# A fused layernorm, causal attention and gated feed-forward kernel: the gate's multiplication, the last unit's diagonal blocks and the second sequence's layernorm take other places in the order of work

## The chip, the core and the metric

The kernel runs on one core of a Trainium2 chip, in a single launch. Its time is device microseconds, the median of several executions. Of one execution there is also a trace, taken by the hardware profiler. It names five engines: PE (TensorE, the matrix multiplications; PEld are its weight loads), DVE (VectorE), ACT (ScalarE), POOL (GpSimd) and SP (SyncE, which here issues nearly all transfers). Microseconds are written us.

## The reference

Two sequences of 1024 tokens with 512 features each, in fp32. Cut to what matters:

```python
xn = layernorm(x)                                   # x: (2, 1024, 512)
q, k, v = (xn @ W.T + b  for W, b in (q, k, v))     # 32 heads of 16
scores = q @ k.T / sqrt(16), causal
s = softmax(scores) @ v @ Wo.T + bo                 # the attention
base = xn @ W_base.T + b_base
w = top-2 of softmax(xn @ W_gate.T) over 8 experts, made to sum to 1
g = silu(base + sum_e w_e * (xn @ A_e.T) @ B_e.T)   # rank 16 each
out = x + s * g
```

## The kernel before

**Units and steps.** All of it is in `direct` (`general` is a second version for inputs out of range; it does not run here). A sequence is b = 0 or 1, and each has two chunks of 512 queries, c = 0 or 1. The 32 heads are four groups of eight (oc). A unit is one (b, oc, c), and there are 16. A unit of chunk 0 has 5 steps, one of chunk 1 has 13 steps; together 144 steps, n = 0 to 143, listed in `plan`. The first unit of the second sequence starts at step 72.

**What a step does.** `scores(n)` (L1610 on) multiplies queries and keys of four heads at once into two PSUM tiles s (the matmuls of L1624; 8 or 16 records of 512 or fewer columns), and ACT takes the exponential of each into a tile pt (128x1024, "exps" below). There are two s tiles, so the scores of step n+1 wait for the exps of step n, and three pt tiles, so the second exp of a step also waits until `values` of the step before has read its buffer. `values(n-1)` (L1676) then multiplies the previous step's pt with the values into the accumulators av. `masked(n)` (L1652) sets the upper triangle of diagonal blocks to zero on POOL, with affine_select. Last, `fill(n)` puts other work behind these: a share of the PE work of the tasks (projections of v, q, k, the gate, the output), planned so that every step gets about the same amount, and what goes with it on DVE, ACT and SP.

**Which blocks share a step.** A step takes pieces of key tile by queries, at most 512 columns. `unit_steps` is for all units but the last. `last_steps` (L1291) orders the last unit's 13 steps, n = 131 to 143. Diagonal pieces are those whose key tile and first query tile are the same. In its steps n = 137 and 138 the two pieces (key tile k0 with 384 columns, key tile k0+2 with 128 columns) are both diagonal.

**What sets the order inside `fill`** (L1513 on). The engines run their instructions in the order in which the program records them; `fill` records: 1. all of `turns` that is due; 2. the PE tasks with their DVE additions (a product's PSUM tile is emptied by such an addition; there are two of these tiles, so each product waits for the addition of the last but one); 3. `splits`; 4. all of `later` that is due (L1574); 5. `urgent` (`place_urgent`, which places queries and keys by DMA); 6. tasks without PE work, such as the layernorm, the sums of inputs and the routing. A task of the sixth kind may take its turn only when DVE is not behind by the planner's estimate (`enough`), unless its due step has come. `later` entries that wait for a DMA have an estimate of when it lands (`landed`).

**The gate** (`gate_task`, L887). The 512x512 block product is made by seven products (p1, p2, p6, p7, p5, p3, p4; Strassen's form) that leave four blocks of g. As each is complete, `final` puts `squash` into `later`: ACT makes sg = tanh(g/2) in a single buffer, and `multiply` (DVE, g = (sg + 1) * g) goes into `later` for the next step. If the next squash comes while a multiply is still pending, it is done first. There are four gates (b, c), with four blocks each: 16 tanh and 16 multiplications.

**The layernorm of a chunk** (`layernorm_task`, L293). SP loads x, DVE takes statistics of four tiles (bn_stats), normalizes four tiles and transposes them in 32x32 blocks (8 instructions, sq); each half goes to HBM (`store`, scr<-sq) and comes back in another order (`place`, four transfers xnT<-scr). The chunk (1,0) may begin from step 28 and is due at step 60 (s0 - 12 with s0 = 72). Its xnT is first used by the projection v of (1,0), which follows the queries and keys ("qk", 0, 1, 3) in the fixed order of stages.

Of the kernel before, what the change touches and what calls it, by code (L numbers as in the profile page):

```python
# [18 lines left out]
P = 128  # L19
# [78 lines left out]
def direct(ctx, tc, sound, x, wq, wk, wv, wo, wb, wa, wg, wB, bq, bk, bv, bo, bb, out):  # L98
# [28 lines left out]
    def chunk_tile(b, c):  # L127
        return sb.tile([P, TT, D], F32, tag="x", bufs=1, name=f"x_{b}_{c}")
# [63 lines left out]
    def load_rest():  # L192


        def by_rows(w):
            return w.rearrange("(kc p) o -> p kc o", p=P)

        for dst, src in (
            (wag_sb[:, :, 0:ER], by_rows(wa)),
            (wag_sb[:, :, ER:], by_rows(wg)),  # L200
            (wB_sb, wB),
            (bb_sb, bb.partition_broadcast(P)),
            (bo_sb, bo.partition_broadcast(P)),
        ):
            sp.dma_start(out=dst, in_=src)
# [42 lines left out]
    turned_at, now = {}, [0]  # L248
# [44 lines left out]
    def layernorm_task(b, c):  # L293


        xt = chunk_tile(b, c)
        for i in range(NS):
            i0 = c * C + i * P
            sp.dma_start(
                out=xt[i * SQ : (i + 1) * SQ],  # L300
                in_=x[b, i0 : i0 + P].rearrange("(t r) d -> r t d", r=SQ),
            )
        if b == 0:
            load_rest()
        tiles = [xt[:, t] for t in range(TT)]
        for _ in range(3 if b else 1):
            yield WAIT
        s = yield from statistics(tiles, True)
        if b:
            yield WAIT  # L310
        for t in range(0, TT, 2):
            normalize(tiles[t : t + 2], s[0][:, t : t + 2], s[1][:, t : t + 2])
            yield PAUSE
        if b:
            yield WAIT
        xnT = sb.tile([P, KC, C], F32, tag="xnT", bufs=3, name=f"xnT_{b}_{c}")
        for k0 in range(0, KC, 2):
            sq = sb.tile([P, 2, NS, TT, SQ], F32, tag="sq", bufs=1, name="sq")
            for t in range(TT):
                yield PAUSE  # L320
                ve.transpose(
                    out=sq[:, :, :, t],
                    in_=tiles[t][:, k0 * P : (k0 + 2) * P].rearrange(
                        "p (k q d) -> p k q d", k=2, q=NS
                    ),
                )
            scr = dram.tile([NS, SQ, 2, NS, TT * SQ], F32, tag="scr", name="scr")

            def store(sq=sq, scr=scr, place=None):
                sp.dma_start(  # L330
                    out=scr.rearrange("i d k q m -> (i d) (k q m)"),
                    in_=sq.rearrange("p k q t r -> p (k q t r)"),
                )
                if place:
                    landed(place, now[0] + 3)

            def place(k0=k0, scr=scr):
                for q in range(NS):
                    sp.dma_start(
                        out=xnT[q * SQ : (q + 1) * SQ, k0 : k0 + 2].rearrange(  # L340
                            "d k (i m) -> d k i m", i=NS
                        ),
                        in_=scr[:, :, :, q].rearrange("i d k m -> d k i m"),
                    )
                if k0:
                    turned_at[b, c] = now[0] + int((sp.landing() - sp.now) / 3.4)

            if not b:
                store()
                place()  # L350
                yield WAIT
                continue
            later.append((now[0] + b, lambda s=store, p=place: s(place=p)))
            for _ in range(0 if k0 else 1 + b):
                yield WAIT
        xnTs[b, c] = xnT
# [527 lines left out]
    def block_of(t):  # L884
        return lambda i, j: t[:, 2 * i : 2 * i + 2, BK * j : BK * j + BK]

    def gate_task(k):  # L887

        _, b, c = stages[k]
        gt = sb.tile([P, TT, D], F32, tag="g", bufs=1, name=f"g_{b}_{c}")  # L890
        away = (b, c) != (NB - 1, NC - 1)
        kept = dram.tile([P, TT, D], F32, tag="kept_g", name="kept_g") if away else None
        stored, multiplied = [], []
        g = block_of(gt)

        def more(ps, i, j, start):
            for t in range(2):
                matmul(
                    ps[:, t * BK : t * BK + BK],
                    lhsT=hwTs[b, c][:, :, 2 * i + t],  # L900
                    rhs=wB_sb[:, BK * j : BK * j + BK],
                    start=start and t == 0,
                    stop=t == 1,
                )

        def final(i, j):

            def squash():
                for x in [x for x in later if x[1].__name__ == "multiply"]:
                    later.remove(x)  # L910
                    x[1]()
                sg = sb.tile([P, 2, BK], F32, tag="tmp", bufs=1, name="sg")
                act.activation(sg, g(i, j), AF.Tanh, scale=0.5)
                later.append((now[0] + 1, lambda: multiply(sg)))
                later[-1][1].__name__ = "multiply"

            def multiply(sg):
                ve.scalar_tensor_tensor(g(i, j), sg, 1.0, g(i, j), ALU.add, ALU.mult)
                if away:
                    later.append((now[0] + 1, store))  # L920
                    return
                multiplied.append((i, j))
                if len(multiplied) == 4:
                    for t in range(TT):
                        gs[b, c * TT + t] = gt[:, t]

            def store():
                sp.dma_start(out=block_of(kept)(i, j), in_=g(i, j))
                stored.append((i, j))
                if len(stored) == 4:  # L930
                    g_tiles[b, c] = kept

            costs[squash] = (0.65, now[0] + 2)
            later.append((now[0] + 1, squash))

        yield from block_task(k, g, final, more)
# [212 lines left out]
        if posted.count(t) == 2:  # L1149
            turns.append((now[0] + 1, lambda: turn_last(b, c, t)))  # L1150

    needs = {}

    def landed(f, cap, at=None):

        needs[f] = sp.landing(), cap
        later.append((now[0] + 1 if at is None else at, f))

    turns, turned, posts, posted, later, patient, last_out = [], [], {}, [], [], [], []
# [131 lines left out]
    def last_steps(c):  # L1291

        k0, w = c * TT, C - P
        steps = []
        for par in range(2):
            for kt in range(0, k0, TT):
                for i in range(TT - 1):

                    steps.append([(par, kt + i, 0, w, 0), (par, kt + TT - 1, i * P, P, w)])
        steps += [[(par, k0, 0, w, 0), (par, k0 + 2, 2 * P, P, w)] for par in range(2)]  # L1300
        steps.append([(par, k0 + 1, P, 2 * P, 2 * P * par) for par in range(2)])
        keys = [k0 + TT - 1] + list(range(k0 + TT - 1))
        pieces = [(par, kt, w, P, i % 4 * P) for par in range(2) for i, kt in enumerate(keys)]
        return steps + [pieces[n : n + 4] for n in range(0, len(pieces), 4)]
# [8 lines left out]
    for u in units:  # L1313
        starts[u] = len(plan)
        steps = unit_steps(u[2]) if u != units[-1] else last_steps(u[2])
# [71 lines left out]
    for b in range(NB):  # L1387
        for c in range(NC):
            s0 = starts[b, 0, c]
            xn = [("xnT", b, c)]  # L1390
            if not b and not c:
                room["x"] -= 1
                Task(1, first_task(), 8 * MM, takes={"xnT": 1, "qT": 1, "kT": 1}, uses=xn)
            else:
                Task(
                    s0 - 12 if b else -9, layernorm_task(b, c), 0.0, after=s0 - (44 if c == 0 else 30) if b else -9,
                    takes={"x": 1, "xnT": 1}, frees={"x": 1},
                )
            turned_ = lambda u=(b, c): now[0] > turned_at.get(u, now[0]) + (0 if u[0] else 1)
# [59 lines left out]
            else:  # L1459
                before = starts[b, KC - 1, c] + 2  # L1460
                Task(len(plan) - 7, bases_task(b, c), 0.0, after=before - 12, takes={"xnT": 2})
                n = len(units) - 3
# [50 lines left out]
    def fill(n):  # L1513
# [54 lines left out]
        for x in [x for x in splits if x[0] <= n]:  # L1568
            if room["qT"] and room["kT"] and (calm(1.1) or n >= starts[x[2]] - 5):
# [1 line left out]
                room["qT"] -= 1  # L1571
                room["kT"] -= 1
                x[1]()
        for x in [x for x in later if x[0] <= n]:  # L1574
            if x not in later or x[0] == n and x[1] in patient and enough():
                continue
            lands, cap = needs.get(x[1], (0.0, 0))
            if lands > (begins if x[1] in patient else clock[0] + 1.0) and n < cap:
                continue
            if x[1] in costs and not calm(costs[x[1]][0]) and n < costs[x[1]][1]:  # L1580
                continue
            later.remove(x)
            x[1]()
# [21 lines left out]
    def place_urgent(n):  # L1605
        for x in [x for x in urgent if x[0] <= n]:
            urgent.remove(x)
            x[1]()
# [129 lines left out]
    while late or turns or tasks:  # L1738
        fill(last + 99)
# [463 lines left out]
```

## Time and profile before

| | |
|---|---|
| time, median of 3 (lowest to highest) | 549.01 us (548.78 to 549.1) |
| the profiled execution's own time | 548.63 us |
| its span, first to last instruction | 546.8 us |
| busy PE, DVE, ACT, POOL | 536.9, 333.0, 351.7, 117.9 us |
| granted TensorE clock, mean | 0.998 |
| transfers | 78.11 MB, mean 143 GB/s |
| exps (pt<-s) | 288, mean 1025 ns |
| masks (pt<-pt on POOL) | 224, mean 501 ns |

The span is what lies between the first and the last instruction; the profiled execution took 1.8 us more than its span. PE counts as busy while a matmul waits inside its group for a buffer, so its 98% hides short stalls: they are found by the distance from one step's first score matmul to the next step's, set against the work in the step. A projection or values matmul of the program stands as two records in the trace, so "p x32" is 16 matmuls; a score matmul stands as one.

### The profile page before, as it was taken

What the parts mean: (1) busy time and instruction counts of PE and PEld (TensorE: products, weight loads), DVE (VectorE), ACT (ScalarE), POOL (GpSimd) and SP (SyncE); (2) the same over time, 40 slices, a digit from 0 to 9 for tenths busy, and PEclk for the clock granted to TensorE, in tenths of its full rate; (3) what the DMA queues carried; (4) which work ended last, traced back from release to release, by engine and by line L of the source; (5) the groups of instructions that cost most, each with busy time, mean ns of one, the idle gap of its engine ahead of it and who ended that gap; (6) DMA issues with size and microseconds to landing.
All of it is one profiled execution on the core that took longest, in us unless ns stands there. A gap on an engine that the chain in (4) does not pass through costs nothing.

```text
span 546.8 us, 19460 instructions
## 1 busy us (share of the span) xinstructions
PE 536.9 (98%) x8411; PEld 278.3 (51%) x8411; DVE 333.0 (61%) x692; ACT 351.7 (64%) x390; POOL 117.9 (22%) x249
## 2 busy tenths in 40 slices
PE   8999999999999999999999999999999999999994
PEld 8435444554455544454645554454545554455562
DVE  4435586665575975576379766575176553648842
ACT  2437754776776867657667756657668767777531
POOL 2213401020134411030123321130123331020500
PEclk9999999999999999999999999999999999999999
DMA  8734357356527376813646545640123221652301
GB/s 262 183 101 159 133 161 233 99 177 197 175 99 230 120 243 209 220 42 100 199 153 197 187 131 176 198 137 23 64 99 123 86 75 46 232 172 86 99 22 66
DMA packets 66798, 78.11 MB, mean 143 GB/s; under 512 B 9880, under 2 KB 51872, under 8 KB 66064
## 3 DMA queue, kind: packets, MB, share of 16 engines
q1 hardware_dynamic: 66688, 76.78, 44.1%
q8 instruction: 68, 1.11, 0.8%
q14 instruction: 26, 0.21, 0.1%
q10 hardware_dynamic: 16, 0.00, 0.0%
HBM read 45.34 MB, written 19.37 MB: 118 GB/s over the span
## 4 chain that ended last, share of the span: by engine, by line
PE 95%; DVE 2%; ACT 1%; issue 0%; POOL 0%; ACTq 0%; POOLq 0%; DVEq 0%
PE av L1676 26%; PE p L257 23%; PE s L1624 18%; PE q L257 14%; PE ph L257 3%; PE pv L257 3%; PE po L257 2%; PE pk L257 1%; PE pq L257 1%; ACT pt L56 1%; PE warm L212 1%; PE pq_first L385 1%; PE h L257 1%; DVE g L56 1%; PE pk_first L385 1%
## 5 line engine op out<-in xcount | busy, mean ns | idle before, releaser
L56 ACT ACTIVATE pt<-s 128x1024 f32<-128x1024 f32 x288 | 290.4, 1025 | 151.8 <-PE s L1624 144.8
L1652 POOL TENSOR_SCALAR_AFFINE_SELECT pt<-pt 128x256 f32<-128x256 f32 (+1 forms) x224 | 108.6, 501 | 405.4 <-ACT pt L56 404.8
L1676 PE MATMUL av<-pt,v 128*32 128x512 f32 (+3 forms) x1680 | 155.7, 467 | 0.4 <-DVE v L56 0.2
L1624 PE MATMUL s<-qT,kT 32*128 32x512 f32 (+3 forms) x1616 | 108.2, 363 | 0.7 <-ACT pt L56 0.5
L1624 PEld LDWEIGHTS s<-qT,kT 32*128 32x128 f32 x1616 | 62.0, 183 | 59.4 <-issue 34.9
L1676 PEld LDWEIGHTS av<-pt,v 128*32 128x32 f32 x1680 | 41.1, 108 | 54.6 <-issue 38.8
L257 PE MATMUL p<-wt,asum 128*32 128x256 f32 x864 | 52.6, 379 | 0.0
L257 PE MATMUL q<-asum,wqk 128*32 128x256 f32 x832 | 51.1, 379 | 0.0
L257 PEld LDWEIGHTS p<-wt,asum 128*32 128x32 f32 x864 | 28.5, 110 | 26.4 <-issue 11.2
L257 PE MATMUL q<-xnT,wqk 128*32 128x256 f32 x624 | 39.5, 379 | 0.0
L257 PEld LDWEIGHTS q<-asum,wqk 128*32 128x32 f32 x832 | 26.8, 110 | 23.7 <-issue 7.2
L56 DVE TENSOR_TENSOR g<-p,g 128x512 f32<-128x512 f32 x20 | 13.8, 690 | 26.6 <-PE p L257 26.5
L257 PEld LDWEIGHTS q<-xnT,wqk 128*32 128x32 f32 x624 | 20.2, 110 | 18.5 <-issue 6.6
L56 DVE SCALAR_TENSOR_TENSOR kf<-q,kf 128x256 f32<-128x256 f32 x39 | 16.5, 424 | 21.3 <-PE q L257 20.6
L257 PE MATMUL p<-w,xnT 128*32 128x256 f32 x448 | 27.4, 379 | 0.0
L257 PE MATMUL p<-w,asum 128*32 128x256 f32 x320 | 20.8, 379 | 0.0
L257 PEld LDWEIGHTS p<-w,xnT 128*32 128x32 f32 x448 | 14.9, 110 | 10.6 <-issue 3.3
L257 PEld LDWEIGHTS ph<-wag_sb,xnT 128*32 128x32 f32 x512 | 15.3, 110 | 3.9 <-issue 3.0
L257 PE MATMUL ph<-wag_sb,xnT 128*32 128x136 f32 x512 | 16.6, 279 | 0.0
L56 DVE TENSOR_TENSOR x<-p,x 128x512 f32<-128x512 f32 x15 | 10.3, 688 | 10.3 <-PE p L257 10.2
L257 PE MATMUL po<-wo,oT 128*32 128x512 f32 x128 | 16.5, 592 | 0.0
L56 DVE TENSOR_TENSOR qT<-qf,qT 128x512 fp32r<-128x512 f32 x15 | 10.4, 696 | 9.4 <-ACT qT L56 9.4
(150 smaller groups left out, 565.8 us busy)
## 6 DMA issues: line engine op xcount, KB each, us to landing
wt<-kept SPq DMA_DIRECT2D x36, 256.0 KB
qT<-qT SPq DMA_DIRECT2D x30, 256.0 KB
x<-in_x_dram SPq DMA_DIRECT2D x16, 256.0 KB
kept<-wqk SPq DMA_DIRECT2D x16, 256.0 KB
wqk<-kept SPq DMA_DIRECT2D x4, 1024.0 KB
kT<-kf SPq DMA_DIRECT2D x30, 128.0 KB
scr<-sq SPq DMA_DIRECT2D x6, 512.0 KB
xnT<-scr SPq DMA_DIRECT2D x24, 128.0 KB
```

The costliest lines, as they stand in the source:

```text
L56: return getattr(self.engine, name)(*args, **named)
L212: nc.tensor.matmul(warm[:, n % 4 * P : n % 4 * P + P], lhsT=ident, rhs=ident, start=True, stop=True)
L257: nc.tensor.matmul(o[j : j + 32], lhsT=lhsT[:, j : j + 32] if len(lhsT.shape) == 2 else lhsT[:, j // 32], rhs=rhs, start=start, stop=stop,)
L385: nc.tensor.matmul(ps[:, cols], lhsT=w[:, k, :], rhs=xnT[:, k, cols], start=k == 0, stop=k == KC - 1)
L1624: nc.tensor.matmul(ss[s // 2][:, s % 2, col : col + w], lhsT=keys[rows, kt % TT * P : kt % TT * P + P], rhs=q[rows, halves * par + half_, ...
L1652: nc.gpsimd.affine_select(out=d, in_=d, compare_op=ALU.is_ge, fill=0.0, base=0, pattern=[[0, d.shape[1]], [1, P]], channel_multiplier=-1,)
L1676: nc.tensor.matmul(avs_now[par][32 * s : 32 * s + 32, q0 : q0 + w], lhsT=vs[b, kt][:, h * VS - HD * par : h * VS - HD * par + HP], rhs=pt[ ...
```

## The change

- `squash` puts `multiply` into `turns` and no longer into `later`. It is recorded at the start of the next step's `fill`, behind that step's `values` and ahead of the DVE additions of its products; before, it came behind them.
- In `last_steps` each diagonal piece is paired with one that isn't. For each half of the heads, the last of the three earlier steps gives its second piece away and takes the diagonal piece of key tile k0+2; the piece that it gave goes with the diagonal of k0 in a step that now directly follows. The four steps with one diagonal piece are then n = 133, 134, 137 and 138. The matmuls are the same.
- The layernorm of (1,0) is due at s0 - 25 = 47 in place of 60. (The chunk (1,1) keeps s0 - 12.)
- The `place` of a layernorm is named in `behind`. When `later` is worked off, such entries come last, and `urgent` is worked off ahead of each: xnT<-scr goes behind the placing of queries and keys on the SP queue.

```diff
@@ layernorm_task, store
                 if place:
+                    behind.append(place)
                     landed(place, now[0] + 3)
@@ gate_task, final
             def squash():
-                for x in [x for x in later if x[1].__name__ == "multiply"]:
-                    later.remove(x)
+                for x in [x for x in turns if x[1].__name__ == "multiply"]:
+                    turns.remove(x)
                     x[1]()
                 sg = sb.tile([P, 2, BK], F32, tag="tmp", bufs=1, name="sg")
                 act.activation(sg, g(i, j), AF.Tanh, scale=0.5)
-                later.append((now[0] + 1, lambda: multiply(sg)))
-                later[-1][1].__name__ = "multiply"
+                turns.append((now[0] + 1, lambda: multiply(sg)))
+                turns[-1][1].__name__ = "multiply"
@@
-    needs = {}
+    needs, behind = {}, []
@@ last_steps
                     steps.append([(par, kt + i, 0, w, 0), (par, kt + TT - 1, i * P, P, w)])
-        steps += [[(par, k0, 0, w, 0), (par, k0 + 2, 2 * P, P, w)] for par in range(2)]
+            steps.append([(par, k0, 0, w, 0), steps[-1][1]])
+            steps[-2][1] = (par, k0 + 2, 2 * P, P, w)
@@ tasks
                 Task(
-                    s0 - 12 if b else -9, layernorm_task(b, c), 0.0, after=s0 - (44 if c == 0 else 30) if b else -9,
+                    s0 - (12 if c else 25) if b else -9, layernorm_task(b, c), 0.0, after=s0 - (44 if c == 0 else 30) if b else -9,
@@ fill
-        for x in [x for x in later if x[0] <= n]:
+        for x in sorted((x for x in later if x[0] <= n), key=lambda x: x[1] in behind):
+            if x[1] in behind:
+                place_urgent(n)
             if x not in later or x[0] == n and x[1] in patient and enough():
                 continue
```

## The prediction

> **What bounds it now.** I read the page first: busy times and the chain that ended last.
>
> ```profile
> PE 536.9 (98%) x8411; PEld 278.3 (51%) x8411; DVE 333.0 (61%) x692; ACT 351.7 (64%) x390; POOL 117.9 (22%) x249
> PE 95%; DVE 2%; ACT 1%; issue 0%; POOL 0%; ACTq 0%; POOLq 0%; DVEq 0%
> ```
>
> PE sets the end nearly everywhere. The change takes no matmul away: in the built program the 32-column products are the same, 8 of them stand in other steps. So time can come only from steps in which PE waits. To find them I set the distance between the first score matmuls of neighbouring steps against the work between them. A full step (16 products, 32 records) takes 3.39 us and one with half of these 2.53, so a record of 256 columns costs 0.86 / 16 = 0.054; with 24 records it is 2.96, and 3.02 where the scores come in two pieces. By these numbers, the start (to step 5) and the tail (from step 141) aside, waits of 0.2 us or more stand in five places, and four of them lie where the change works.
>
> Place 1, step 48, in the timelines of DVE, ACT and PE:
>
> ```profile
> 199.54 0.69 DVE L56 TENSOR_TENSOR g<-p,g 128x512 f32<-128x512 f32 x1 [0.36 <-PE p L257]
> 200.15 0.68 DVE L56 SCALAR_TENSOR_TENSOR g<-sg,g 128x512 f32<-128x512 f32 x1
> ...
> 200.86 0.63 ACT L56 ACTIVATE sg<-g 128x512 f32<-128x512 f32 x1 [2.00 <-DVE g L56]
> 201.40 1.92 ACT L56 ACTIVATE pt<-s 128x1024 f32<-128x1024 f32 x2
> ...
> 199.41 0.74 PE L1624 MATMUL s<-qT,kT 32*128 32x512 f32 x8
> ...
> 202.80 1.30 PE L1624 MATMUL s<-qT,kT 32*128 32x512 f32 x8
> ...
> 206.75 0.74 PE L1624 MATMUL s<-qT,kT 32*128 32x512 f32 x8
> ```
>
> The multiplication g<-sg,g stands behind an addition that waits for PE. The next tanh needs its buffer sg and sits in front of the exps of step 47; these end at 203.32, and the scores of step 48, begun at 202.80, take 1.30 in place of 0.74. The step has 3.95 us for 3.39 of work: **0.56 lost**.
>
> Place 2, steps 129 and 130, the same in the last gate:
>
> ```profile
> 478.41 0.69 DVE L56 TENSOR_TENSOR qT<-qf,qT 128x512 fp32r<-128x512 f32 x1 [2.63 <-ACT qT L56]
> 479.68 0.69 DVE L56 TENSOR_TENSOR g<-p,g 128x512 f32<-128x512 f32 x1 [0.58 <-PE p L257]
> 480.29 0.93 DVE L56 SCALAR_TENSOR_TENSOR g<-sg,g 128x512 f32<-128x512 f32 x1
> ...
> 481.31 0.63 ACT L56 ACTIVATE sg<-g 128x512 f32<-128x512 f32 x1 [1.11 <-DVE g L56]
> ```
>
> From 479.98 to 487.71 the two steps take 7.73 for 6.0 of work: 1.73 lost.
>
> Place 3, step 51: step 50 had only 16 records to fill it (the row at 211.69), since v of (1,0) could not begin, so its exps end at 213.00, after the scores of step 51 begin:
>
> ```profile
> 211.69 1.05 PE L257 MATMUL q<-xnT,wqk 128*32 128x256 f32 x16
> 212.67 1.16 PE L1624 MATMUL s<-qT,kT 32*128 32x384 f32 x16
> ```
>
> Step 51 takes 3.82 (to 216.49) where such a step takes 3.44 elsewhere: 0.4 lost.
>
> Place 4, steps 138 to 140, from 508.85 to 518.96: 10.11 for 2.60 + 2.60 + 2.95 = 8.15 of work, 1.96 lost. POOL and ACT there:
>
> ```profile
> 507.87 2.08 POOL L1652 TENSOR_SCALAR_AFFINE_SELECT pt<-pt 128x256 f32<-128x256 f32 x4 [19.73 <-ACT pt L56]
> 510.90 2.61 POOL L1652 TENSOR_SCALAR_AFFINE_SELECT pt<-pt 128x256 f32<-128x256 f32 x4 [0.94 <-ACT pt L56]
> ...
> 510.99 1.02 ACT L56 ACTIVATE pt<-s 128x1024 f32<-128x1024 f32 x1 [0.22 <-PE av L1676]
> 512.84 1.02 ACT L56 ACTIVATE pt<-s 128x1024 f32<-128x1024 f32 x1 [0.82 <-PE s L1624]
> 514.55 1.02 ACT L56 ACTIVATE pt<-s 128x1024 f32<-128x1024 f32 x1 [0.69 <-PE av L1676]
> ```
>
> Four masks a step end late, av waits for them, and the second exp waits for av's buffer. The fifth place (0.2 in step 24) is a DVE backlog of the routing, which stays.
>
> **The change, part by part.**
>
> *Multiplication ahead, place 1.* In the built order it now stands directly behind the copies of av, which end at 199.18. It would end at 199.86, the tanh run from 199.9 (ACT is free from 198.87), the exps of step 47 from 200.5 to 202.4, before PE reaches 202.80. The whole wait goes: **-0.56**. The next tanh then starts at 202.4 and ends at 203.0, before the scores that the following exps need (203.5); nothing new is late.
>
> *Place 2.* The multiplication moves ahead of g<-p,g: 479.10 to 479.8, or 480.0 if it takes 0.93 again beside a mask. The addition ends at 480.5 to 480.7, the tanh starts 0.55 to 0.8 earlier than 481.31, and the exps, scores, masks and av behind it move by as much, since each waits for the one before. I take **-0.65**; the two steps then still lose 1.1.
>
> *Elsewhere.* Sixteen multiplications, each 0.68, now stand ahead of an addition that frees a product's PSUM tile. At steps 27 and 109 that addition waits for PE longer than 0.68 anyway. At 105 DVE had a hole of that size in front of it. At 131 the next product into the tile begins over 1 us later. At step 24 the cover is gone: the addition would end at 122.6 in place of 121.96, and its tile is wanted at 122.57. **+0.1** (0 to 0.3).
>
> *Layernorm of (1,0) earlier.* Its four statistics (0.85 each), four normalizations (0.55) and eight transposes (0.42), 9 us of DVE in all, move up by 3 to 5 steps and change places with the sums of w_out. Summed by rows, DVE has 4.7, 2.6, 4.1 and 1.7 us to do in steps 41 to 44, against 4.9, 3.1, 3.2 and 2.0 now; steps are 3.4, and the late ones (the sums behind p5) free a tile that is wanted 3 us later. So nothing for PE. The last xnT transfer is recorded in step 45 rather than 49, v starts in step 50, and steps 54 and 57 give up the 8 records each that they now have beyond 32. Work stays the same, and the wait of step 51 goes: **-0.4** (0 if v's inputs come late).
> On SP the queries of step 46 now stand behind both den, both avs, one scr store, two weight and gate transfers and dens. By the issue times before, SP reaches them at about 189.8, against 189.16, with some 1.5 MB to move; in the window 189.16 to 196.01 the transfers made 309 GB/s, 5 us. They land at 193 to 194.5, wanted at 196.01. The xnT transfers (3.5 us of issue) stay behind them. I cost it at nothing, with 0 to 1.5 as bounds.
>
> *Diagonal pieces.* Two masks a step in place of four at 137 and 138. The second exp of step 138 no longer waits 0.22 and ends at 511.78; scores of 139 end at 512.58 in place of 512.81; av takes its 1.0 and is done at 513.6, so the second exp of 139 runs 513.63 to 514.65 in place of 514.55 to 515.57. From there all is as now, 0.92 earlier: **-0.9**. More is not to be had, because the exps' own round is the limit there: from one step's last exp (508.75) to the next one's (511.78), 3.03 for 2.60 of PE work. Bounds: -0.3 (masks stay slow) to -1.2.
> At 133 and 134 two masks each are added. The last exps end at 496.66 and 499.68, av begins at 497.49 and 500.51: 0.83 for a mask of 0.41, the commonest duration. Beside DVE sums that read two SBUF tiles (x_last<-x_last,y) the masks of steps 137 to 139 took 0.55 to 0.95. The Trainium skill's GPSIMD Engine Reference (Specifications) has the reason: GpSimd shares its SBUF interfaces with VectorE, in contention with DVE instructions that have two SBUF inputs. The trace agrees, and it speaks against the new places, for steps 133 and 134 hold four such sums each; by it the masks end at up to 0.95 behind the exps, 0.12 late at most. I leave this in the range.
>
> **Sum:** -0.56 - 0.65 + 0.1 - 0.4 - 0.9 = -2.4. The profiled execution took 548.63 (span 546.8), so 546.2 on its own terms; the median of the runs is 549.01, 0.38 above it, and the forecast for the median is **546.6**. Its own range is 545.4 to 547.6. About 0.2% (1.1 us) is what a measurement of this kernel can tell from no change.
>
> **Rivals.**
> 1. *Given back.* The exps' round is 3.0 us beside steps of 3.0 to 3.4, so a step that starts earlier may wait for ACT a little later. For: at place 4 it takes half. Against: steps 49 and 131 to 137 hold no wait. If half of the 2.4 is lost: 547.8. Chance 0.12.
> 2. *Queries late at step 46*, the SP queue as above. If DMA runs as in the xnT transfers (181 GB/s from 198 to 200 rather than 309), 1.5 MB, begun at 188, take 8 us: they land near 197 and cost 1 to 1.5: 547.9. Chance 0.07.
> 3. *Slower: the multiplication blocks DVE.* DVE takes its instructions in order. At the head of a step the multiplication waits for the tanh, which may stand behind two exps (2.03), and each addition behind it holds a PSUM tile. To end above no change, the sixteen must cost 0.15 each beyond the -2.4, above 550.1 0.22 each; at 0.3 each it is 551.4. For: step 24. Against: at the other gates' steps the tanh ends by 1.4 us into the step, the tile is wanted over 2 us in. Chance 0.06.
> 4. *v is not ready at step 50*, so the third part does nothing or stalls on xnT: 547.0 to 547.6, within the forecast's range. The built order, with v in step 50, speaks against it.
>
> **Chances.** Forecast 0.75, rivals 1 and 2 0.19, rival 3 0.06. Rivals 1 and 2 lie about the bound of 547.9, half on each side: faster 0.84, same 0.10, slower 0.06. The range for 8 in 10 is 545.3 to 548.0.
>
> **What would show it.** Right: step 48 at 3.4 us with the tanh no longer waiting for g; step 51 at 3.4; steps 129 and 130 together near 7.1; steps 138 to 140 near 9.2, with the second exps no longer waiting for av; PE's distance between steps unchanged elsewhere. Wrong: a new wait of scores for qT at step 46, of products for g or v at steps 24 and 50 to 57, or of av for masks at 134 and 135.

## The result, and the profile after

| | before | after |
|---|---|---|
| median (lowest to highest), 6 executions each | 549.06 us (548.78 to 549.52) | 546.32 us (545.78 to 546.6) |
| ratio of the times, 95% interval | | 0.9949 (0.9939 to 0.9959) |
| profiled execution, its span | 548.63, 546.8 us | 546.6, 544.9 us |

The kernel became 2.7 us faster; 546.6 was forecast. The profiled execution of after is the slowest of its six and that of before lies 0.4 below its median, so these two differ by 2.0 only.

The lines of `scores`, `masked` and `values` moved down by four: L1624, L1652 and L1676 are now L1628, L1656 and L1680. First the page of after, the busy times and the chain that ended last:

```profile
PE 534.6 (98%) x8411; PEld 277.9 (51%) x8411; DVE 333.9 (61%) x692; ACT 351.8 (65%) x390; POOL 117.8 (22%) x249
...
PE 92%; DMA 2%; ACT 2%; DVE 2%; issue 1%; SPq 0%; ACTq 0%; DVEq 0%
```

The instructions are as many as before on every engine. PE's busy time fell by 2.3 us for the same 8411 matmuls, since a matmul that waits inside its group counts as busy (the scores of step 48 stand with 1.30 us before and 0.74 after). New in the chain is DMA with 2%; some of that becomes important below.

As for the prediction, I set the distance between the first score matmuls of neighbouring steps, before against after, and kept what differs by 0.05 or more. The last column is the same in a kernel whose profile shows no wait for a DMA at that place (`e4_loads_behind`, below).

| place | predicted | after | without the DMA wait |
|---|---|---|---|
| 1: step 48, 3.96 to 3.39 | -0.56 | -0.57 | -0.57 |
| 2: steps 129 and 130, 7.73 to 7.31 | -0.65 | -0.42 | -1.38 |
| step 24, 4.04 to 4.12 | +0.1 | +0.08 | +0.08 |
| step 44, 3.45 to 3.57 | 0 | +0.12 | +0.12 |
| 3: steps 50 to 57 | -0.4 | -0.37 | -0.37 |
| 4: steps 138 to 140, 10.11 to 9.32 | -0.9 | -0.79 | -0.79 |
| sum | -2.4 | -1.95 | -2.91 |

Steps 123 and 124 are left out, because they only exchange 0.09 (-0.09 and +0.08). The start, up to the first score, and the end, from the scores of the last step on, are no part of this either: their lengths change from execution to execution. The start took 14.59 us before and 14.96 after, the end 15.49 and 15.15; two executions of one and the same kernel further below differ by 0.88 in the start and by 0.23 in the end.

**Place 1** in the timeline of after, all engines (start, duration, engine, line, operation, count, and in brackets the idle time before and what ended it):

```profile
199.15 0.68 DVE L56 SCALAR_TENSOR_TENSOR g<-sg,g 128x512 f32<-128x512 f32 x1
...
199.86 0.63 ACT L56 ACTIVATE sg<-g 128x512 f32<-128x512 f32 x1 [0.44 <-DVE g L56]
...
199.96 0.74 PE L1628 MATMUL s<-qT,kT 32*128 32x512 f32 x8
200.10 0.69 DVE L56 TENSOR_TENSOR g<-p,g 128x512 f32<-128x512 f32 x1 [0.27 <-PE p L257]
...
203.35 0.74 PE L1628 MATMUL s<-qT,kT 32*128 32x512 f32 x8
```

The multiplication now stands ahead of the addition that waits for PE. The tanh waits 0.44 for it in place of 2.00, and the scores of step 48 take 0.74 in place of 1.30.

**Place 2**, the same view at the last gate:

```profile
478.64 0.68 DVE L56 SCALAR_TENSOR_TENSOR g<-sg,g 128x512 f32<-128x512 f32 x1
...
479.31 0.69 DVE L56 TENSOR_TENSOR g<-p,g 128x512 f32<-128x512 f32 x1
...
479.71 0.64 ACT L56 ACTIVATE sg<-g 128x512 f32<-128x512 f32 x1
...
480.89 1.11 SPq L72 DMA_DIRECT2D qT<-qT  x2
...
482.89 0.74 PE L1628 MATMUL s<-qT,kT 32*128 32x256 f32 x16
...
486.91 0.79 PE L1628 MATMUL s<-qT,kT 32*128 32x384 f32 x16 [0.89 <-DMA qT<-qT]
```

The tanh begins while the addition still runs, 0.11 us behind the head of step 129 (1.33 before). The step that begins at 482.89 then lasts 4.02, and its end is another wait. The chain of waits of that stretch (start, duration, what) names it:

```profile
480.35 0.53 ACT qT L56
...
480.89 5.88 DMA qT<-qT
...
486.91 0.79 PE s L1628 x14
```

The queries of the last unit are issued at 480.89 and have landed at 486.77, while PE could have begun step 131 at 485.95. Before, they were issued at 482.49 and wanted at 487.71; no wait was seen.

**Place 3**, PE in steps 50 and 51: v begins in step 50 (the row at 212.55), which is full now, and step 51 takes 3.45 (to 216.97, 3.82 before).

```profile
211.69 1.05 PE L257 MATMUL q<-xnT,wqk 128*32 128x256 f32 x16
212.55 1.05 PE L257 MATMUL p<-w,xnT 128*32 128x256 f32 x16
213.53 0.80 PE L1628 MATMUL s<-qT,kT 32*128 32x384 f32 x16
```

**Place 4**, POOL and then ACT. Two masks a step, and the second exps come directly behind the first (x2 in one row, no wait between) where they waited up to 0.69 for av:

```profile
510.03 0.53 POOL L1656 TENSOR_SCALAR_AFFINE_SELECT pt<-pt 128x256 f32<-128x256 f32 x1 [1.55 <-ACT pt L56]
511.03 0.41 POOL L1656 TENSOR_SCALAR_AFFINE_SELECT pt<-pt 128x256 f32<-128x256 f32 x1 [0.47 <-ACT pt L56]
```

```profile
508.94 2.02 ACT L56 ACTIVATE pt<-s 128x1024 f32<-128x1024 f32 x2 [0.99 <-PE s L1628]
511.75 2.12 ACT L56 ACTIVATE pt<-s 128x1024 f32<-128x1024 f32 x2 [0.79 <-PE s L1628]
515.03 2.11 ACT L56 ACTIVATE pt<-s 128x1024 f32<-128x1024 f32 x2 [1.17 <-POOL pt L1656]
```

Steps 138, 139 and 140 take 2.58, 2.91 and 3.83 (3.00, 3.56 and 3.56 before): the first two gave 1.07, and 140 took 0.27 of it back.

**Step 44**, not foreseen. On DVE three sums of w_out, on POOL four masks beside them:

```profile
187.19 2.22 DVE L56 TENSOR_TENSOR w_out<-w_out 128x512 f32<-128x512 f32 x3
```

```profile
188.13 2.27 POOL L1656 TENSOR_SCALAR_AFFINE_SELECT pt<-pt 128x256 f32<-128x256 f32 x4 [2.05 <-ACT pt L56]
```

The single masks are 0.74, 0.85, 0.40 and 0.40. Before, POOL was busy for 1.99 in their place (one of 0.91 and three of 0.41, which overlap a little), against 2.27 here. So the contention that the prediction looked for at steps 133 and 134, where no step rose, shows here.

### The profile page after: what moved, and what is told of

Read it like the earlier page. It is cut to its first block, busy times and chain, and to the rows that moved or that the text cites. A ratio compares the mean times of both kernels' runs of the same rounds, so it can differ in the third digit from the quotient of the medians.

```text
span 544.9 us, 19464 instructions
## 1 busy us (share of the span) xinstructions
PE 534.6 (98%) x8411; PEld 277.9 (51%) x8411; DVE 333.9 (61%) x692; ACT 351.8 (65%) x390; POOL 117.8 (22%) x249
## 4 chain that ended last, share of the span: by engine, by line
PE 92%; DMA 2%; ACT 2%; DVE 2%; issue 1%; SPq 0%; ACTq 0%; DVEq 0%
PE av L1680 25%; PE p L257 22%; PE s L1628 18%; PE q L257 14%; PE ph L257 3%; PE pv L257 3%; PE po L257 2%; ACT pt L56 1%; PE pq L257 1%; PE pk L257 1%; DMA qT<-qT 1%; DMA x<-in_x_dram 1%; PE pk_first L386 1%; DMA kept<-w_gate 1%; PE pq_first L386 1%
## 5 line engine op out<-in xcount | busy, mean ns | idle before, releaser
L1656 POOL TENSOR_SCALAR_AFFINE_SELECT pt<-pt 128x256 f32<-128x256 f32 (+1 forms) x224 | 108.5, 499 | 403.5 <-ACT pt L56 402.8
L1680 PE MATMUL av<-pt,v 128*32 128x512 f32 (+3 forms) x1680 | 154.4, 467 | 0.4 <-DVE v L56 0.2
L1628 PE MATMUL s<-qT,kT 32*128 32x512 f32 (+3 forms) x1616 | 107.3, 363 | 0.9 <-DMA qT<-qT 0.9
L1628 PEld LDWEIGHTS s<-qT,kT 32*128 32x128 f32 x1616 | 61.5, 183 | 59.2 <-issue 33.2
L1680 PEld LDWEIGHTS av<-pt,v 128*32 128x32 f32 x1680 | 41.3, 108 | 53.6 <-issue 38.6
L56 DVE TENSOR_TENSOR v<-p,v 128x512 f32<-128x512 f32 x15 | 10.3, 684 | 10.5 <-PE p L257 10.4
```

The source lines that it names most:

```text
L56: return getattr(self.engine, name)(*args, **named)
L1628: nc.tensor.matmul(ss[s // 2][:, s % 2, col : col + w], lhsT=keys[rows, kt % TT * P : kt % TT * P + P], rhs=q[rows, halves * par + half_, ...
L1656: nc.gpsimd.affine_select(out=d, in_=d, compare_op=ALU.is_ge, fill=0.0, base=0, pattern=[[0, d.shape[1]], [1, P]], channel_multiplier=-1,)
L1680: nc.tensor.matmul(avs_now[par][32 * s : 32 * s + 32, q0 : q0 + w], lhsT=vs[b, kt][:, h * VS - HD * par : h * VS - HD * par + HP], rhs=pt[ ...
```

## The experiments

Ratios are to runs of the kernel before on the same chip, with their 95% interval.

### The multiplication alone

Before, with the first part of the change only:

```diff
-                later.append((now[0] + 1, lambda: multiply(sg)))
-                later[-1][1].__name__ = "multiply"
+                turns.append((now[0] + 1, lambda: multiply(sg)))
+                turns[-1][1].__name__ = "multiply"
```

> The kernel before with the multiplication alone put into turns. Theory (the three parts act each at their own steps and add up): step 48 falls by 0.57 us to 3.39, steps 129 and 130 together by 0.4 from 7.73, step 24 rises by 0.1, all else as before: about 548.15 us against 549.05. Rival (given back): the steps fall and others rise, the time stays within 0.3 us of before.

547.36 us (546.95 to 547.68), ratio 0.9968 (0.9956 to 0.998): 1.6 gained, of the 2.7 of the whole change. Step 48 gave 0.56. Steps 129 and 130 gave 0.17 and 1.23, 1.40 together: twice the 0.65 of the prediction, and far more than the 0.4 expected here, which is what after's profile shows with its wait. So the time is 0.8 below the expected 548.15. Steps 138 and 139 took 0.23 back. Here no wait for the queries stands in the profile. The timeline of this kernel, all engines:

```profile
479.45 0.69 DVE L56 TENSOR_TENSOR g<-p,g 128x512 f32<-128x512 f32 x1
...
479.85 0.64 ACT L56 ACTIVATE sg<-g 128x512 f32<-128x512 f32 x1
...
483.03 0.75 PE L1624 MATMUL s<-qT,kT 32*128 32x256 f32 x16
...
486.09 0.80 PE L1624 MATMUL s<-qT,kT 32*128 32x384 f32 x16
```

The tanh begins 0.4 after the addition g<-p,g does, not after its end. So it does not need that addition: it works on another block of g, which was complete before, and needs from DVE only the buffer sg, which the multiplication frees.

### The diagonal pieces alone

```diff
-        steps += [[(par, k0, 0, w, 0), (par, k0 + 2, 2 * P, P, w)] for par in range(2)]
+            steps.append([(par, k0, 0, w, 0), steps[-1][1]])
+            steps[-2][1] = (par, k0 + 2, 2 * P, P, w)
```

> The kernel before with the new pairs of the last unit alone. Theory: steps 138 to 140 together fall by 0.8 us from 10.12, steps 48, 51, 129 and 130 stay: about 548.25 us. Rival (masks slow beside two-input sums at 133 and 134): steps 134 or 135 rise by 0.2 or more and the time falls by less than 0.5.

548.48 us (547.7 to 549.64), ratio 0.9987 (0.9978 to 0.9996). Steps 138, 139 and 140 changed by -0.41, -0.64 and +0.43, together -0.62 where 0.8 was expected; nothing rose at 134 and 135. Its profiled execution was the slowest of eleven, and the chain of waits shows a reason (step 55 lasted 1.12 longer):

```profile
223.66 7.85 DMA w<-in_wv_dram
...
231.65 0.64 PE p L257 x8
```

A weight tile took 7.85 us from its issue. The change does nothing at that place in this kernel, so I take it for one execution's late transfer; the other ten are not traced.

### The layernorm alone

`behind`, and the due step 47 in place of 60, on before:

```diff
-                    s0 - 12 if b else -9, layernorm_task(b, c), 0.0, after=s0 - (44 if c == 0 else 30) if b else -9,
+                    s0 - (12 if c else 25) if b else -9, layernorm_task(b, c), 0.0, after=s0 - (44 if c == 0 else 30) if b else -9,
```

> The kernel before with the earlier layernorm and its placing behind queries alone. Theory: steps 50 to 57 together fall by 0.37 us, step 44 rises by 0.12, step 48 stays at 3.9: about 548.8 us. Rival: the wait of step 48 came from the layernorm's transposes on DVE and not from the place of the multiplication; then step 48 falls here too, and the time is about 548.2.

549.18 us (548.15 to 550.0), ratio 1.0003 (0.9994 to 1.0012): nothing, a miss of 0.4. The trace has both halves of it. Steps 50 to 57 gave 0.37 as forecast, and step 44 took 0.44. There, masks of 0.62, 0.85 and 0.85 stand beside the w_out sums. Timelines of POOL and of DVE:

```profile
187.94 2.24 POOL L1655 TENSOR_SCALAR_AFFINE_SELECT pt<-pt 128x256 f32<-128x256 f32 x3 [2.04 <-ACT pt L56]
```

```profile
187.01 0.68 DVE L56 SCALAR_TENSOR_TENSOR g<-sg,g 128x512 f32<-128x512 f32 x1
187.61 2.30 DVE L56 TENSOR_TENSOR w_out<-w_out 128x512 f32<-128x512 f32 x3
```

The earlier layernorm moves these sums beside the masks. How far depends on the other parts: in after the sums begin at 187.19 and only two masks are slow. Step 48 keeps its 3.96 here, so the layernorm's transposes were not its cause.

### The loads of the last output behind the queries

After, with the first loads of x and g (xr, gr, four of 256 KB) of the output (1,0) put behind the queries of the last unit on SP:

```diff
-        load()
-        load()
+        if b:
+            later.append((starts[units[-1]] - 1, lambda: (load(), load())))
+        else:
+            load()
+            load()
```

> The changed kernel, with the first four loads of the output of chunk (1,0) (xr and gr, 1 MB) issued behind the last unit's queries and not ahead of them. Theory (after the change the scores of step 131 wait for the queries, whose transfer stands behind these loads on the DMA engines): the wait of 0.9 us ahead of step 131 goes, step 130 takes about 3.1 us in place of 4.02, and the time is about 545.4 us. Rival: the transfer takes its 5.9 us whatever stands ahead, or the loads come late for steps 131 and 132 in turn: no change, 546.3.

> The changed kernel with the loads of the output of chunk (1,0) behind the last queries (due 47), once more, beside the two runs with due 48. Theory: step 45 is longer than 3.40 us by 0 to 1 us for queries that come late, so 0.3 to 1 us slower than the run with due 48. Rival: no difference.

First run: 546.3 us (545.92 to 546.92), ratio 0.9951 (0.9937 to 0.9965). Step 130 fell from 4.02 to 3.06 and the wait was gone; every other step is as in after. Second run: 546.12 (545.94 to 547.56), ratio 0.995 (0.9936 to 0.9963), again 3.06. So the 0.96 at step 130 of after's profile is the queries' transfer, and nothing else is hidden there. But the 545.4 expected of the first run did not come, and the ratio is that of after (0.9949): over its executions the wait seems to cost after less than its profile shows. The step 45 expected to be longer in the second run is not longer in its profile; its median lies 0.23 and 0.34 above the two kernels with due 48 below, with intervals that overlap.

### After again

> The changed kernel once more, for a second profile beside its first. Theory (the 0.9 us for which step 131 waited for its queries come from transfers whose landing differs from one execution to the next): step 130 takes anything from 3.06 to 4.02 us, and executions without the wait are about 0.9 us shorter than those with it. Rival (the wait belongs to the kernel): step 130 takes 4.0 us again.

547.2 us (545.76 to 549.74), ratio 0.9963 (0.9951 to 0.9975). In its profile step 130 takes 3.56 and the scores wait 0.4 for qT, where the first profile had 4.02 and 0.9. The wait is real and its size is a matter of the execution. This profile shows a second one: step 45 takes 3.61 in place of 3.40. The chain there goes through the queries of step 46, issued at 191.93 (191.16 in the first profile) and landed 4.93 later, just when PE could have begun. On this chip the change is worth 2.1 us (549.26 before), on the first one 2.7. The span of four us between executions of this set is more than these waits; what the longest of them wait for is not traced.

### Without `behind`

```diff
-                    behind.append(place)
```

> The changed kernel without the entry in behind: the layernorm's xnT transfers keep their place in the list, and the last four of them go ahead of the queries of step 46. Theory (the queries are issued 3.2 us later, at about 194.4 us, and land at about 198): the scores of step 46 wait 1 to 2 us, the time is about 547.8 us. Rival (the queries have more room than the SP queue shows): no wait, 546.3 us.

549.15 us (548.14 to 550.63), ratio 0.9998 (0.9987 to 1.0009). On the same chip after made 0.9963, so this one line is worth some 2 us by the medians, at the upper end of the 1 to 2 expected. From the list of PE's waits, and from the chain:

```profile
PE s L1627 <- DMA qT<-qT: 2.3, 1, 2.3
```

```profile
196.00 3.00 DMA qT<-qT
...
199.14 0.86 PE s L1627 x5
```

The queries of step 46 stand behind the four xnT transfers on SP (3.44 us of issue) and go out at 196.00, only 0.8 before PE could begin that step. In after's first profile they go out at 191.16, and step 46 has no wait. The profiled execution here is the slowest of its twelve: step 45 lasts 2.38 longer than before, and step 46, whose exps are late with it, another 1.61. The 4.0 of this profile are thus more than the line costs as a rule.

### No masks in the last unit

After, without the 16 masks of the last unit: its scores are then not causal. What is left out is POOL's work only.

```diff
         cols = [col for _, kt, q0, _, col in pieces if kt * P == c * C + q0]
+        if (b, oc, c) == units[-1]:
+            cols = []
```

> The changed kernel without the masks of the last unit (16 instructions of POOL are left out, so the last unit is not causal). Theory (after the change the exps' own round is what steps 138 to 140 wait for, not the masks): the three steps stay at 2.58, 2.91 and 3.83 us within 0.1, and the time within 0.2 of 546.3. Rival (masks beside two-input sums of DVE still hold av back): the three steps fall by 0.3 us or more together.

547.14 us (546.26 to 547.52), ratio 0.9959 (0.9947 to 0.9972). On this chip after made 547.2, so the time did not change. Steps 138 and 139 did not change either, and 140 fell by 0.1 (3.83 to 3.72; after's second profile has 4.09). ACT in this kernel:

```profile
511.09 2.12 ACT L56 ACTIVATE pt<-s 128x1024 f32<-128x1024 f32 x2 [0.79 <-PE s L1628]
514.37 2.11 ACT L56 ACTIVATE pt<-s 128x1024 f32<-128x1024 f32 x2 [1.17 <-PE s L1628]
```

From the exps of 511.09 to those of 514.37 it is 3.28, exactly as with masks (511.75 to 515.03 in after), though there the profile names a mask as what ended the 1.17 of idling. The mask was only the last of several to come. So masks no longer set the time at place 4. What is left is the round of scores and exps: here the exps wait 0.79 and 1.17 for scores. That it is this round is concluded by exclusion and not shown by a run of its own.

Up to step 131 this kernel gives SP, DVE and ACT the same instructions in the same order as after, so it serves as a third profile of after there. Step 130 takes 3.06, without a wait for the queries, and step 45 takes 3.60, much as in the second, though here the chain names no transfer.

### The sums of w_out later

The kernel with the loads behind, and the sums of w_out allowed from step 40 in place of 34, to take them from beside the masks of step 44:

```diff
-                        (20, 48)[n], combine_task(name), 0.0, after=(9, 34)[n], takes={"xnT": 1},
+                        (20, 48)[n], combine_task(name), 0.0, after=(9, 40)[n], takes={"xnT": 1},
```

> The changed kernel with the loads of the output of chunk (1,0) behind the last queries, and with the task that makes the sums of w_out beginning at step 40 in place of 34, so that these sums run in step 48, where POOL has no masks, and not in steps 43 and 44. Theory (step 44 waits 0.12 us for masks that take 0.74 to 0.85 in place of 0.41 beside the sums): step 44 falls from 3.57 to 3.45, and the time is 545.4 to 546.2 us. Rival: the w_out loads now ahead of the queries of step 46 make its scores wait, and the time rises by 0.5 or more.

549.72 us (548.75 to 553.37), ratio 1.0023 (1.0004 to 1.0041). The masks beside step 44 are 0.41 again and the step gave the 0.12 back. But the loads of w_out moved too. From the list of PE's waits and the timeline of SP:

```profile
PE s L1631 <- DMA qT<-qT: 2.1, 1, 2.1
...
PE p L257 <- DMA w<-in_wv_dram: 1.3, 1, 1.3
```

```profile
190.83 0.56 SPq L72 DMA_DIRECT2D w_out<-in_wo_dram  x1
...
192.26 0.57 SPq L72 DMA_DIRECT2D w_out<-in_wo_dram  x1
...
194.92 1.16 SPq L72 DMA_DIRECT2D qT<-qT  x2
```

The queries of step 46 go out at 194.92 and step 45 lasts 2.16 longer. Saving 0.12 on POOL cost 2.1 on SP: rival 2's mechanism at the place for which the prediction had it. The two w_out loads ahead of the queries are 1.13 of issue; the issues of dens (1.46, 0.48 in after) and of the first xnT transfers (3.94, 2.65 and 3.59 in after's two profiles) are longer too, and why is not known. Step 55 also lasts 1.53 longer, for a weight tile that landed 7.33 after its issue.

### The layernorm due one step later

After with `s0 - (12 if c else 24)`, with and without the loads behind, and without them once more:

> The changed kernel with the layernorm of (1,0) due one step later (48 in place of 47) and the loads of the output of chunk (1,0) behind the last queries. By the built order the second store of the layernorm (scr, 512 KB) and its xnT transfers then stand behind the queries of step 46, the sums of w_out run in steps 41 and 42, and v still begins in step 50. Theory (what is left of the waits comes from transfers ahead of queries): no wait at steps 44 to 46, step 130 at 3.06 us, step sums about 3.1 us below before, and less spread than the changed kernel. Rival: xnT, landing 7 us later, makes step 50 wait.

> The changed kernel with the layernorm of (1,0) due one step later, and nothing else. Theory: no wait at steps 44 to 46 as in the run before it, while step 130 waits for queries by 0 to 1 us, differently from one execution to the next; 0.3 to 0.6 us slower than the run before it. Rival: as fast as that one, so that the loads ahead of the last queries cost nothing on the mean.

> The kernel with the layernorm of (1,0) due at 48 (everything else as after), a second time. In the traces so far SP's issue of the weight transfer wt<-kept ahead of the last unit's queries takes 0.45 us in this kernel and 1.1 to 1.8 in those with the layernorm due at 47, and the scores of step 131 wait for the queries only where it took 1.6 or more with the loads of xr and gr behind it. Theory: the order of this kernel brings the short issue and step 44 back to 3.45 us, so both are seen again: no wait for qT, median 545.5 to 546.2 where the kernel before has 549.1. Rival: the issue's duration is a matter of the execution, and the gain over after is chance: the issue takes over 1 us, step 130 over 3.06, median 546.3 to 547.2 with a spread of 2 us or more, as after had in its second set of executions.

| kernel | median (lowest to highest) | ratio |
|---|---|---|
| due 48, loads behind | 545.89 (545.59 to 546.33) | 0.9935 (0.9922 to 0.9949) |
| due 48 | 545.78 (545.39 to 546.21) | 0.9937 (0.9923 to 0.9951) |
| due 48 again | 545.53 (545.44 to 546.52) | 0.9937 (0.9923 to 0.995) |

In all three, step 44 takes 3.45 and step 130 3.06; every other step is as in after's first profile. v still begins in step 50, and xnT is not late. The wait at step 130 expected of the second kernel is not in its profile, and it is no slower than the first: the loads behind bring nothing here, as the rival had it. The third run met its theory. All three medians lie below those of the four sets with due 47 (546.1 to 547.2); it is the lowest seen, but the intervals overlap with that of after, so that it beats after is likely and not shown. The two executions of one kernel (due 48, 545.39 and 546.52 in the profiled execution) agree in every step but the last; the second starts its first score 0.88 later, and its end is 0.23 longer.

The timeline of SP ahead of the last unit's queries, due 48 (second run), and then after:

```profile
477.03 0.45 SPq L72 DMA_DIRECT2D wt<-kept  x1
477.53 0.50 SPq L72 DMA_DIRECT2D xr<-in_x_dram  x1
...
478.58 1.04 SPq L72 DMA_DIRECT2D xr<-in_x_dram  x1
479.67 0.47 SPq L72 DMA_DIRECT2D gr<-kept_g  x1
481.14 1.11 SPq L72 DMA_DIRECT2D qT<-qT  x2
```

```profile
476.77 1.76 SPq L72 DMA_DIRECT2D wt<-kept  x1
478.58 0.46 SPq L72 DMA_DIRECT2D xr<-in_x_dram  x1
...
480.11 0.47 SPq L72 DMA_DIRECT2D gr<-kept_g  x1
```

One issue in this sequence takes longer than its 0.45. In after it is the first, 1.76 (1.60 in the second profile), and the 1 MB of loads starts 4.31 ahead of step 130 (482.89). With due 48 it is a later one, 1.28 or 1.04, and the loads start 5.61 ahead of it (483.14), while the queries go out 2.0 ahead in both. The wait for qT was seen only where the first issue took 1.6 or more with the loads behind it. With the multiplication moved and the loads ahead of the queries there are seven profiles:

| profile | first issue | loads start ahead of step 130 | step 130 |
|---|---|---|---|
| after | 1.76 | 4.31 | 4.02 |
| after again | 1.60 | 4.46 | 3.56 |
| no masks (same order up to here) | 1.12 | 4.94 | 3.06 |
| multiplication alone, without `behind`, due 48 twice | 0.45 each | 5.61 to 5.62 | 3.06 each |

In these, the wait is the longer the later the loads start. The length of the first issue is a matter of the execution at least among the first three, which have one order. The expectation of the third run gives 1.1 to 1.8 for the kernels with due 47; the layernorm alone, the one without `behind` and the one with the later sums have due 47 too, and took 0.45. Why it is 0.45 in some is open: between after and due 48, the order on SP differs only around steps 43 to 49, some 80 steps earlier. Open too is the rest of the gain of due 48. The profiles show 0.12 at step 44, and the 0.2 at step 45 of after's second profile is not there; the medians of the two kernels with the loads behind, where neither waits for qT, lie 0.2 to 0.4 apart.

## Why the prediction was right, and where it was off

**Place 1** (-0.56) came as worked out, also alone: -0.57 and -0.56. **Step 24** was +0.08 of +0.1. **Rival 3**, the multiplication that blocks DVE, falls: the first experiment has all sixteen in their new places, and no step but 24 grew by more than 0.05 until the last unit, apart from 124, which took over 0.08 of what 123 lost.

**Place 2** is the term that was mis-sized. It failed in this step: "The addition ends at 480.5 to 480.7, the tanh starts 0.55 to 0.8 earlier". I let the tanh wait for g<-p,g because that was the addition ahead of the multiplication, but the tanh is of another block and waits for sg alone. So it began 1.2 earlier in its step, and the two steps gave 1.4. "The two steps then still lose 1.1" is wrong as well: without the wait for the queries they take 6.35 for 6.0 of work. In after's own profile most of the surplus went to **the queries of the last unit**, which I had not priced at all. They are scaled by ACT behind that tanh, so they too go out 1.6 earlier, but now 5.06 us ahead of the time at which they are wanted (5.22 before) and directly behind 1 MB of loads. They took 5.88. In both runs with the loads behind the wait is gone, though the first issue took 1.55 and 1.71 there; the seven profiles show that with the loads ahead it comes only in some executions.

**Rival 2** had the right mechanism at another step. At step 46, where I costed it at nothing, after's first profile has no wait, since `behind` holds the xnT transfers back; in its second profile the queries landed at 196.86 and cost 0.21. So the margin of 1.5 to 3 us that I read from the issue times was used up there. My issue time was off by 1.4 (191.16 in place of 189.8; 0.4 of this is the later start), and by 2.1 in the second profile. Without `behind` the cost is 2 us by the medians, and with 0.5 MB of w_out loads ahead 2.1 in the profile.

**Place 3** (-0.4) gave 0.37, but I counted only DVE time when I wrote "So nothing for PE". The sums of w_out moved next to masks, and step 44 took 0.12, and 0.44 where the layernorm was moved alone. The GPSIMD Engine Reference of the Trainium skill (Specifications) has the rule: GpSimd and VectorE share SBUF interfaces, and DVE instructions with two SBUF inputs contend. The trace agrees: 0.74 and 0.85 beside such a sum, 0.40 behind it. The prediction applied it to the places that masks moved to, not to those that sums moved to.

**Place 4** (-0.9) gave 0.79. The kernel without masks shows that masks are no longer the limit there; that the exps' round is, as I wrote, is what remains. **Rival 1**, given back, shows in part: step 140 takes 0.27 back (0.43 with the pieces alone).

The sum of the steps is -1.95 in after's profile against -2.4. The median fell by 2.7: the two profiled executions lie on the unfavourable sides of their medians, by 0.3 and 0.4. Against the profiles that have no DMA wait (-2.9), place 2 gave 0.73 more than forecast, and places 3 and 4 with step 44 gave 0.26 less. That the median came within 0.3 of the forecast is therefore partly luck: a gain twice as large as I gave to place 2 was cut down by terms that I had put at nothing, step 44 and queries that land late.

## What to carry to other kernels

Before you price a wait, ask of each instruction in the chain which operand it really needs: an in-order neighbour is not a dependency, and here that was worth twice the forecast. When a step starts earlier, look at the transfers that it waits for: their lead in time must grow with it, and small loads issued just ahead of them can become a cost (0.5 and 1.0 us in two of seven profiles here). A sum of engine times does not show what two engines do to each other, so check also what moved instructions come to stand beside.

## What the runs showed of the hardware

- The same transfer takes different times in different executions. The last unit's queries needed 5.88 us from issue in one profile of after and were 0.4 late instead of 0.9 in another; a weight tile took 7.85 us and made PE wait 0.9 in the kernel with the diagonal pieces alone, and before shows no such wait.
- SP's issue of one and the same weight transfer, ahead of the last unit's queries, took from 0.45 to 1.76 us. In three executions with the same order of instructions up to there it took 1.76, 1.60 and 1.12 (after twice, and without masks); two profiles of due 48 have 0.45 each.
- A mask of 128x256 on POOL commonly took 0.40 to 0.41 us. It took 0.62 to 0.85 beside sums of w_out on DVE, and 0.91 beside the multiplication g<-sg,g of before. These lengthened ones end 0.26 to 0.27 us after the end of that DVE instruction (in after at step 44, sums of w_out that end at 188.60 and 189.42, and masks that end at 188.87 and 189.68). The same holds for all 35 masks of this shape in before that took over 0.5 us: each of them ends so behind a DVE instruction that was already running when it began.
